# Two graph layers on one core: fp8 copies on GpSimd, layer 1's sums re-dealt over the steps, weights in one transfer, split gathers and filler matmuls

## The chip, the core and the metric

The kernel runs on one core of one Trainium2 chip. Its engines are named as the profile names them: PE is TensorE (matmuls; PEld its weight loads), DVE is VectorE, ACT is ScalarE, POOL is GpSimd, SP is SyncE. Every load of this kernel is issued by POOL, except the weights, which SP issues as it does the stores. The metric is the device time of one execution in microseconds (us). Three runs of the kernel before took 259.87, 260.9 and 263.14 us; the median is 260.9.

## What is computed

Two layers over a graph of 4096 nodes with 64 features. `adj` is a 0/1 matrix of 4096 x 4096 in float32 (64 MB), in which about one entry in 256 is set.

```python
# layer 0: the last 100 neighbours of a row count, each half of the next one
support = input @ weight
mask = (adj != 0); rank = cumsum(mask, axis=1); deg = rank[:, -1:]
k = minimum(deg, 100); pos = rank - (deg - k)
w = mask * where(pos > 0, 0.5 ** (k - pos), 0)
x = layernorm(x + (w @ support + bias))
# layer 1
deg = clip(sum(adj, axis=1) + 1, 1)
h = (adj @ x + x) / deg
out = relu(concat([x, h], axis=1) @ W + b)
x = layernorm(x + out / maximum(norm(out, axis=1), 1e-12))
```

Layer 1 needs the rows of layer 0's result, so its product `adj @ x` can only be summed over nodes that layer 0 has finished.

## The kernel before, in words

**Tiles and steps.** `adj` is cut into 8 slabs g of 512 rows (the output nodes) by 8 blocks k of 512 columns (the neighbours). A tile A[g][k] is 128 partitions x 4 x 512, loaded transposed on the host and cast from float32 to bfloat16 by the DMA (512 KB in SBUF). There are 64 steps; step i works on slab g = i // 8 and block k = 7 - i % 8, as layer 0's ranks run from the last column back.

**A step.** `weigh` makes the weights of a tile: 32 small matmuls (L294 on the tile with `tri`, L303 with the number of later neighbours `near`) into PSUM, from which ACT (L310) and DVE (L311) each turn one half into `w`. `gather` (L321) multiplies `w` by x in four matmuls, one step later, into the accumulator acc0. `count` (L264) counts the neighbours of tiles ahead, DVE adds them up as `cs` (L274, L276), `spread` (L282) sums them over the later columns and ACT makes `near` (L284). Tiles are counted in chunks: of one in slab 0, of one and two in slab 1, of two in slabs 2 and 3, of four from slab 4 on; a chunk is counted during the chunk before it, so step 30 counts the tiles of steps 32 to 35.

**Loads.** `load_next` in step i loads the tile of step i + 6 (six go ahead of step 0). The pool `a16` has 23 slots, so a load waits on POOL (L111) for a slot. POOL's other work stands in the same queue: the loads of x, the split of x into two halves of float16 (L224) in steps 0 to 7, and adding layer 0's bias (L254).

**Layer 1's sums.** Once layer 0 has finished slab k, the block k of any slab can be summed: `second` (L330), four matmuls per tile. `some_sums` does at most four matmuls a step (QUOTA), from a hand-written list `jobs` of (slab, first block, one past the last); a tile may be taken at step i if i >= 8 (k + 1) + 7 and it has been weighed. All the blocks of one job are added in acc1, an accumulator with one buffer, and `evict_part` then copies or adds it into `part[g]` on DVE (L368, L365). Jobs of the old list take 27 tiles in steps 15, 23 to 27, 31 to 34, 39 to 52 and 55 to 57. The other 37 tiles are summed in the tail.

**Kept tiles.** Tiles of slabs 0 to 3 with k >= 4 are needed again only in the tail. `keep_next` copies them to fp8 (0 and 1 are exact) in halves of 128x1024 and so frees their bf16 slot: one half a step from step 9 on but for every eighth, three on ACT (L346) to one on DVE (L344), behind the step's own work.

**Epilogue of layer 0** for slab g, by hooks in the steps after i = 8 (g + 1): in i, ACT copies acc0 (`first_hT`, L426); i + 1, PE multiplies by the weights (L432); i + 2, DVE adds x and makes the statistics (L439, L419, L421); i + 3 and i + 4, the root on ACT (L390) and DVE (L396 to L400) and the normalised x1 (L459); i + 5 and i + 6, its two halves x1hl (L464, L468, L471) and the transposes (L476); i + 7, the products with layer 1's weights (`first_pu`, L487); i + 8, `first_c1` (L496, L497). The weights themselves are scaled and split in three bfloat16 parts by DVE in steps 6 to 8 (L230 to L249).

**The tail** after step 63: layer 0's epilogue for slab 7, the sums that are left (`own`), and layer 1's epilogue in units of two slabs: `last_hT` (DVE adds part[g], L612), `last_pz` (PE, L640), `last_z` (DVE, L647), squares on ACT (L654, L655), `last_ss` (DVE, L662), the root on POOL (`last_rn`, L410), `last_y` (DVE L681, then the add on POOL, L684), `last_mv` (statistics, L419 and L421), `last_r` (POOL: L408 to L702), `last_o` (eight outputs on ACT, L722) and the stores. Slab 7 comes last, in halves of 256 columns (`own_half`, `half_hT`).

**Order.** The order of each engine's instructions is the program's, written out by hand; each engine runs its own list in that order and waits by semaphores.

```python
    def evict_part(g):
        acc = acc1.pop(g)
        if g in part:
            nc.vector.tensor_tensor(part[g], acc, part[g], ALU.add)
        else:
            part[g] = const.tile([P, R], F32, name=f"part_{g}")
            nc.vector.tensor_copy(part[g], acc)
...
    jobs = [(0, 0, 2), (1, 0, 2), (2, 0, 2), (3, 0, 3), (2, 2, 4), (0, 2, 4), (1, 2, 4)]
    jobs += [(4, 0, 4), (5, 0, 5), (6, 0, 3)]
```

Of the kernel before, what the change touches and what calls it, by code (L numbers as in the profile page):

```python
# [9 lines left out]
F32 = mybir.dt.float32  # L10
# [30 lines left out]
def adj_resnorm_kernel(  # L41
# [5 lines left out]
    w0: bass.AP,  # L47
    b0: bass.AP,
    w1: bass.AP,
    b1: bass.AP,  # L50
# [18 lines left out]
    D = w0.shape[0]  # L69
# [32 lines left out]
    def load_next(n=1, pieces=1):  # L102
        for _ in range(n):
            s = next(loads, None)
            if s is None:
                return
            g, k = s
            a = a16p.tile([P, KB, R], BF16, tag="a16", name=f"a16_{g}_{k}")
            for h in range(pieces):
                qs = slice(h * KB // pieces, (h + 1) * KB // pieces)  # L110
                nc.gpsimd.dma_start(out=a[:, qs, :], in_=adjT[g, k][:, qs, :])  # L111
            A[g][k] = a
# [14 lines left out]
    load_next(1, pieces=2)  # L127
# [58 lines left out]

    w0_sb = const.tile([P, D], F32, name="w0_sb")
    wn_sb = const.tile([P, D], F32, name="wn_sb")

    w1_sb = const.tile([P, 2 * D], F32, name="w1_sb")  # L190
    w1_parts = const.tile([P, 3, 2 * D], BF16, name="w1_parts")
# [3 lines left out]
    b0_sb = const.tile([P, D], F32, name="b0_sb")  # L195
    b1_sb = epi.tile([P, D], F32, tag="y", name="b1_sb")
# [9 lines left out]
    def load_weights():  # L206
        nc.sync.dma_start(out=w0_sb[0:D, :], in_=w0)
        nc.sync.dma_start(out=w0_sb[D:P, :], in_=w0)
        nc.sync.dma_start(out=b0_sb, in_=b0.partition_broadcast(P))
        for h in range(2):  # L210
            for c in range(2):
                nc.sync.dma_start(out=w1_sb[h * D : (h + 1) * D, c * D : (c + 1) * D], in_=w1[c * D : (c + 1) * D, :])
        nc.sync.dma_start(out=b1_sb, in_=b1.partition_broadcast(P))
        nc.sync.dma_start(out=wn_sb[0:D, :], in_=w1[D : 2 * D, :])
        nc.sync.dma_start(out=wn_sb[D:P, :], in_=w1[D : 2 * D, :])
# [13 lines left out]
    def prepare():  # L229
        nc.vector.tensor_scalar(w0_sb[0:D, :], w0_sb[0:D, :], 2.0**W_EXP, None, ALU.mult)  # L230
        nc.vector.tensor_scalar(w0_sb[D:P, :], w0_sb[D:P, :], 2.0**W_EXP / LO, None, ALU.mult)

    def prepare_last():
        nc.vector.tensor_scalar(wn_sb[D:P, :], wn_sb[D:P, :], 1.0 / LO, None, ALU.mult)
        nc.vector.tensor_scalar(w1_sb[D:P, :], w1_sb[D:P, :], 1.0 / LO, None, ALU.mult)
        for j in range(3):
            nc.vector.tensor_copy(w1_parts[:, j, :], w1_sb)
            if j < 2:
                nc.vector.tensor_tensor(w1_sb, w1_sb, w1_parts[:, j, :], ALU.subtract)

    def prepare_b1():
        for j in range(3):
            nc.vector.tensor_copy(
                b1_parts[j * 32 : j * 32 + 1], b1_sb[j * 32 : j * 32 + 1].unsqueeze(1).to_broadcast([1, TB, D])
            )
            if j < 2:
                high = epi.tile([P, D], BF16, tag="sq", name=f"b1_high_{j}")
                nc.vector.tensor_copy(high, b1_sb)
                nc.vector.tensor_tensor(b1_sb, b1_sb, high, ALU.subtract)  # L249
# [66 lines left out]
    def gather(g, k, w):  # L316
        if k == NK - 1:
            acc0[g] = ps_a.tile([P, R], F32, tag="acc0", name=f"acc0_{g}")
        for q in range(KB):
# [16 lines left out]
    def keep_next(i):  # L336
        if not to_keep:
            return
# [4 lines left out]
        if i % 4 == 3:  # L343
            nc.vector.tensor_copy(kept[g, k][:, qs, :], A[g][k][:, qs, :], saturate=False)  # L344
        else:
            nc.scalar.copy(kept[g, k][:, qs, :], A[g][k][:, qs, :], saturate=False)  # L346
# [4 lines left out]
    jobs = [(0, 0, 2), (1, 0, 2), (2, 0, 2), (3, 0, 3), (2, 2, 4), (0, 2, 4), (1, 2, 4)]  # L351
    jobs += [(4, 0, 4), (5, 0, 5), (6, 0, 3)]
    have = {g: 0 for g in range(NG)}
    acc1 = {}

    todo = [(g, b, b == k0 * KB, b == k1 * KB - 1) for g, k0, k1 in jobs for b in range(k0 * KB, k1 * KB)]
# [5 lines left out]
    def evict_part(g):  # L362
# [3 lines left out]
        else:  # L366
            part[g] = const.tile([P, R], F32, name=f"part_{g}")
            nc.vector.tensor_copy(part[g], acc)  # L368

    def some_sums(i, n):  # L370

        done = None
        while n and todo and done is None and ready(i, todo[0][0], todo[0][1]):
# [4 lines left out]
            have[g] = b // KB + 1  # L378
# [102 lines left out]
    def first_pu(g):  # L481
# [3 lines left out]
        for t in range(TB):  # L485
            for j in range(3):
                nc.tensor.matmul(  # L487
                    pu[:, t, :], lhsT=x1T[:, ts(t, P)], rhs=w1_parts[:, j, :], start=(t, j) == (0, 0), stop=False
                )
# [22 lines left out]
    at(NK - 2, DVE, prepare)  # L512
    at(NK - 1, DVE, prepare_last)
    at(NK, DVE, prepare_b1)
# [23 lines left out]
    pi = ps_m.tile([P, R], F32, tag="m", name="pi")  # L538
    for i in range(12):
        nc.tensor.matmul(pi, lhsT=idle[:, 0:P], rhs=idle, start=True, stop=True)  # L540
    pf = ps_m.tile([P, P], F32, tag="m", name="pf")
# [4 lines left out]

    nc.vector.memset(w0_sb, 0.0)
    load_weights()
    spread(0, NK - 1)
    held = None  # L550
    for c, chunk in enumerate(chunks):
# [7 lines left out]
        for (g, k), share in zip(chunk, shares):  # L559
            i = when[g, k]  # L560
            run(i, ACT)
            run(i, POOL)
            load_next()
# [7 lines left out]
            run(i, "ACT, late")  # L571
            done = some_sums(i, QUOTA)
            if share and share[-1] == ahead[-1]:
                spread(*ahead[-1])

            if i > NK and i % NK:
                keep_next(i)
            if held is not None:
                gather(*held)
# [14 lines left out]
    def own(g, b0, b1):  # L594

        for b in range(b0, b1):
            second(acc[g], g, b, b == have[g] * KB, b == NB - 1)
# [144 lines left out]
    def acc_of(g, tag, rows=R, name=None):  # L742
        return ps_a.tile([P, rows], F32, tag=tag, name=f"acc_right_{name or g}")

    acc.update({5: va[:, 0, :], 2: vb[:, 0, :], 1: va[:, 1, :], 4: vb[:, 1, :]})
    acc[0] = acc_of(0, "acc1")
    last = L * KB
    own(5, 20, 24)
# [10 lines left out]
    own(5, 24, last)  # L759
    own(2, 16, last)  # L760
    own(0, 16, 20)
    first_px(L)
    first_x1T(L)
    own(0, 20, 24)
    own(5, last, NB)
    last_hT(5)
    own(2, last, NB)
    last_hT(2)
    first_pu(L)
    first_c1(L)  # L770
# [3 lines left out]
    own(0, 24, NB)  # L774
    last_z(u)
    last_sq(u, True)
    last_hT(0)
    last_ss(u)
    last_rn(u, True)
    own(1, 16, NB)  # L780
    last_hT(1)
    last_y(u, True)
    own(4, 16, 24)
# [3 lines left out]
    own(4, 24, NB)  # L787
# [3 lines left out]
    last_sq(v, True)  # L791
    last_hT(4)
    last_ss(v)
    last_rn(v, True)
    last_o(u, 0, 8)
    store(u)
    acc[3] = acc_of(3, "acc0")
    own(3, 12, NB)
    last_y(v, True)
    last_hT(3)  # L800
    acc[6] = acc_of(6, "acc1")
    own(6, 12, 20)

    u = unit(4, 3)
    last_pz(u)
    last_mv(v)
    last_r(v, True)
    last_z(u)
    last_sq(u, True)
    last_o(v, 0, 8)  # L810
    store(v)
    own(6, 20, NB)
    last_ss(u)
    last_rn(u, True)
    last_hT(6)
    acc[L, 0] = acc_of(L, "acc0", R // 2, "7a")
    own_half(a_half, 0, NB // 4)

    v = unit(6)
    last_pz(v)  # L820
    own_half(a_half, NB // 4, NB)
    last_y(u, True)
    last_z(v)
    last_sq(v, False)
# [77 lines left out]
```

## Time and profile before

| | us |
|---|---|
| runs: median (lowest to highest) | 260.9 (259.87 to 263.14) |
| profiled execution: its time | 260.26 |
| its span, first to last instruction | 258.4 |
| busy: PE / DVE / ACT / POOL | 215.9 / 179.9 / 147.7 / 77.6 |
| ACT fp8 copies L346: 23 of 1038 ns | 23.9 |
| DVE fp8 copies L344: 9 of 693 ns | 6.2 |
| POOL load issues L111: 65 of 574 ns | 37.2 |
| POOL waiting ahead of L111 | 111.7 |
| last gather (step 63) starts | 203.58 |
| the last slab's last product (L640) starts | 247.12 |
| last output instruction ends | 255.4 |

The profile is of one execution, and its rows carry line numbers of the kernel before. Busy time of PE counts pipelined matmuls whose ends are modelled: a matmul of 512 columns is listed with 0.38 us but the next one starts 0.216 us later. The granted clock was 0.67 of full speed from 10 to 20 us and full from there to the end of the matmuls. In a timeline row the columns are start, duration, engine, line, operation, output <- input, shape and, in brackets, the idle time ahead of it and what ended it.

### The profile page before, as it was taken

What the parts mean: (1) busy time and instruction counts of PE and PEld (TensorE: products, weight loads), DVE (VectorE), ACT (ScalarE), POOL (GpSimd) and SP (SyncE); (2) the same over time, 40 slices, a digit from 0 to 9 for tenths busy, and PEclk for the clock granted to TensorE, in tenths of its full rate; (3) what the DMA queues carried; (4) which work ended last, traced back from release to release, by engine and by line L of the source; (5) the groups of instructions that cost most, each with busy time, mean ns of one, the idle gap of its engine ahead of it and who ended that gap; (6) DMA issues with size and microseconds to landing.
All of it is one profiled execution on the core that took longest, in us unless ns stands there. A gap on an engine that the chain in (4) does not pass through costs nothing.

```text
span 258.4 us, 7468 instructions
## 1 busy us (share of the span) xinstructions
PE 215.9 (84%) x3187; PEld 99.5 (39%) x3187; DVE 179.9 (70%) x471; ACT 147.7 (57%) x210; POOL 77.6 (30%) x129
## 2 busy tenths in 40 slices
PE   8496767679979996998889899998996989999920
PEld 2122224224424432442344234433442636646920
DVE  5666697796797696667957694668577555556773
ACT  5366666687878668656866575447444421064271
POOL 8655471051013240232122422130200000475640
PEclk9779999999999999999999999999999999999995
DMA  5999999999999999599899999996500000000111
GB/s 90 179 238 233 240 214 214 221 219 214 215 221 205 202 188 211 107 212 191 169 148 188 205 215 213 223 212 118 104 0 3 3 0 0 3 22 20 43 41 41
DMA packets 12241, 37.37 MB, mean 145 GB/s; under 512 B 2353, under 2 KB 3377, under 8 KB 12209
## 3 DMA queue, kind: packets, MB, share of 16 engines
q0 software_dynamic: 10128, 35.66, 69.8%
q1 hardware_dynamic: 2080, 1.25, 1.7%
q8 instruction: 25, 0.41, 0.6%
q14 instruction: 8, 0.06, 0.1%
HBM read 69.40 MB, written 1.05 MB: 273 GB/s over the span
## 4 chain that ended last, share of the span: by engine, by line
PE 37%; DMA 23%; DVE 17%; issue 9%; POOL 6%; ACT 6%; POOLq 0%; ACTq 0%; DVEq 0%
DMA a<-in_adjT_dram 23%; PE acc L321 7%; PE acc_part L330 6%; DVE w L311 4%; PE v L294 4%; ACT w L310 4%; PE acc_right L330 3%; PE cnt L264 3%; PE v L303 2%; DVE x L459 2%; POOL a L111 2%; PE pz L640 2%; PE va L330 2%; PE pu L487 2%; PE vb L330 2%
## 5 line engine op out<-in xcount | busy, mean ns | idle before, releaser
L310 ACT ACTIVATE w<-v,less 128x1024 int16<-128x1024 f32 x64 | 71.3, 1114 | 48.3 <-PE v L303 30.1
L311 DVE TENSOR_SCALAR w<-v 128x1024 int16<-128x1024 f32 x64 | 78.2, 1222 | 29.3 <-PE v L303 27.5
L111 POOL DMA_DIRECT2D a<-in_adjT_dram x65 | 37.2, 574 | 111.7 <-PE acc_part L330 36.5
L321 PE MATMUL acc<-w,xhl 128*128 128x512 bf16 x256 | 66.3, 381 | 0.2 <-ACT hT L426 0.2
L321 PEld LDWEIGHTS <-xhl 128*128 128x128 f16 x256 | 24.0, 98 | 36.6 <-issue 12.8
L294 PE MATMUL v<-a,tri 32*32 32x512 bf16 x1024 | 29.7, 390 | 6.3 <-ACT w L310 5.9
L264 PE MATMUL cnt<-a,pick 128*32 128x512 bf16 x256 | 22.9, 393 | 12.6 <-DMA a<-in_adjT_dram 12.2
L330 PEld LDWEIGHTS <-x1hl 128*128 128x128 f16 x224 | 19.6, 98 | 29.3 <-issue 10.4
L303 PE MATMUL v<-near,mine 32*32 32x512 bf16 x1024 | 29.0, 382 | 0.2 <-ACT near L284 0.2
L274 DVE TENSOR_TENSOR cs<-cnt,cs 128x512 bf16<-128x512 f32 x22 | 15.1, 688 | 18.5 <-PE cnt L264 18.5
L330 PE MATMUL acc_part<-a,x1hl 128*128 128x512 bf16 x108 | 28.0, 382 | 0.0
L284 ACT ACTIVATE near<-rep,most 128x512 bf16<-128x512 f32 x30 | 20.5, 683 | 6.6 <-PE rep L282 6.6
L346 ACT CAST a<-a 128x1024 fp8e4<-128x1024 bf16 x23 | 23.9, 1038 | 0.0
L294 PEld LDWEIGHTS <-tri 32*32 32x32 bf16 x1024 | 10.8, 88 | 28.9 <-issue 27.5
L282 PE MATMUL rep<-cs,further 128*128 128x512 bf16 x30 | 11.8, 392 | 9.8 <-DVE cs L274 7.4
L410 POOL TENSOR_TENSOR rn<-ss,power 128x8 f32<-128x8 f32 (+1 forms) x4 | 6.0, 1506 | 34.8 <-DVE ss L664 34.7
L264 PEld LDWEIGHTS <-pick 128*32 128x32 bf16 x256 | 5.3, 94 | 28.6 <-issue 19.4
L330 PE MATMUL acc_right<-a,x1hl 128*128 128x512 fp8e4 (+1 forms) x56 | 12.9, 379 | 0.0
L654 ACT ACTIVATE sq<-z 128x512 f32<-128x512 f32 x3 | 1.9, 630 | 17.2 <-DVE z L647 17.2
L419 DVE BATCH_NORM_STATS2 st_l<-y 128x6 f32<-128x64 f32 x60 | 9.0, 214 | 1.0 <-POOL y L684 0.8
L303 PEld LDWEIGHTS <-mine 32*32 32x32 bf16 x1024 | 9.3, 88 | 0.8 <-issue 0.7
L464 ACT CAST x1hl<-x 128x256 f16<-128x256 f32 x8 | 3.2, 405 | 10.6 <-DVE x L459 10.6
(135 smaller groups left out, 255.8 us busy)
## 6 DMA issues: line engine op xcount, KB each, us to landing
a<-in_adjT_dram POOLq DMA_DIRECT2D x63, 512.0 KB, 9.3
c<-in_x_quads_dram POOLq DMA_DIRECT2D x8, 128.0 KB, 11.8
x<-in_x_dram POOLq DMA_DIRECT2D x8, 128.0 KB, 9.3
out_dram<-o SPq DMA_DIRECT2D x8, 128.0 KB, 1.7
a<-in_adjT_dram POOLq DMA_DIRECT2D x2, 256.0 KB, 4.9
w_sb<-in_L_gnn_W_dram SPq DMA_DIRECT2D x4, 16.0 KB, 10.8
w_sb<-in_L_gnn_weight_dram SPq DMA_DIRECT2D x2, 16.0 KB, 6.2
b_sb<-in_L_gnn_bias_dram SPq DMA_DIRECT2D x1, 32.0 KB, 8.2
```

Source lines behind the costliest of these rows:

```text
L111: nc.gpsimd.dma_start(out=a[:, qs, :], in_=adjT[g, k][:, qs, :])
L264: nc.tensor.matmul(cnt[g][quarters[q], :], lhsT=pick[:, PW - 4 * k : PW - 4 * k + Q], rhs=A[g][k][:, q, :], start=first, stop=last,)
L274: nc.vector.tensor_tensor(new, cnt[g], cs[g], ALU.add)
L282: nc.tensor.matmul(pr, lhsT=further, rhs=cs[g], start=True, stop=True)
L284: nc.scalar.activation(near[g], pr, AF.Relu, bias=most, scale=-1.0)
L294: nc.tensor.matmul(v[e // 2][quarters[q], e % 2, :], lhsT=tri[quarters[e], :], rhs=A[g][k][quarters[e], q, :], start=True, stop=False,)
L303: nc.tensor.matmul(v[e // 2][quarters[q], e % 2, :], lhsT=mine[quarters[e], 4 * k + q, :], rhs=nr[quarters[e], :], start=False, stop=True,)
L310: nc.scalar.activation(w[:, 0:2, :], v[0], AF.Relu, bias=less)
L311: nc.vector.tensor_scalar(w[:, 2:4, :], v[1], -STEP * MAX_NEIGH, 0.0, ALU.add, ALU.max)
L321: nc.tensor.matmul(acc0[g], lhsT=xhl[:, b, :], rhs=w[:, q, :].bitcast(BF16), start=(k, q) == (NK - 1, 0), stop=(k, q) == (0, KB - 1),)
L330: nc.tensor.matmul(acc, lhsT=x1hl[:, b, :], rhs=A[g][b // KB][:, b % KB, :], start=first, stop=last)
L346: nc.scalar.copy(kept[g, k][:, qs, :], A[g][k][:, qs, :], saturate=False)
```

## The change

It has seven parts:

- `keep_next` runs on POOL alone, ahead of the step's load, from step 3 on and only for tiles already weighed: one half a step, steps 3 to 34.
- `jobs` lists single blocks in any order; 20 jobs take 39 tiles in steps 15, 16, 23 to 26, 30 to 35 and 37 to 63. A slab's first eviction is an ACT copy, the later ones are DVE adds.
- The tail sums what is left (`left`, 25 tiles) in a new order, with other accumulators; the last unit of layer 0 (`first_pu`, `first_c1` of slab 7) comes later in it.
- The four weight arrays become one array of 128x384, put together on the host and loaded by one SP transfer in step 1; POOL scales and splits it in steps 6 and 9 to 12.
- The first tile is loaded in one transfer, not two halves.
- In a step that ends a chunk and has no sums, half of the gather goes ahead of `spread`.
- Filler matmuls: 14 instead of 12 ahead of the start, and 4, 2, 4 and 3 more around the first counts and step 0.

```diff
-    load_next(1, pieces=2)
+    load_next()
...
     def load_weights():
-        nc.sync.dma_start(out=w0_sb[0:D, :], in_=w0)
...
-        nc.sync.dma_start(out=wn_sb[D:P, :], in_=w1[D : 2 * D, :])
+        nc.vector.memset(wts[:, 0:1], 0.0)
+        nc.sync.dma_start(out=wts, in_=weights)
...
-    def prepare_last():
-        nc.vector.tensor_scalar(wn_sb[D:P, :], wn_sb[D:P, :], 1.0 / LO, None, ALU.mult)
...
+    def prepare_w1(j):
+        if j == 0:
+            low = wts[D:P, D : 4 * D]
+            nc.gpsimd.tensor_scalar(low, low, 1.0 / LO, None, ALU.mult)
+        nc.gpsimd.tensor_copy(w1_parts[:, j, :], w1_b1)
+        if j < 2:
+            nc.gpsimd.tensor_tensor(w1_b1, w1_b1, w1_parts[:, j, :], ALU.subtract)
...
-    def gather(g, k, w):
+    def gather(g, k, w, q0=0, q1=KB):
...
     def keep_next(i):
-        if not to_keep:
+        if i < 3 or not to_keep or when[to_keep[0][0:2]] >= i:
             return
...
-        if i % 4 == 3:
-            nc.vector.tensor_copy(kept[g, k][:, qs, :], A[g][k][:, qs, :], saturate=False)
-        else:
-            nc.scalar.copy(kept[g, k][:, qs, :], A[g][k][:, qs, :], saturate=False)
+        nc.gpsimd.tensor_copy(kept[g, k][:, qs, :], A[g][k][:, qs, :], saturate=False)
...
-    jobs = [(0, 0, 2), (1, 0, 2), (2, 0, 2), (3, 0, 3), (2, 2, 4), (0, 2, 4), (1, 2, 4)]
-    jobs += [(4, 0, 4), (5, 0, 5), (6, 0, 3)]
+    jobs = [(0, [0]), (1, [0])]
+    jobs += [(2, [0, 1]), (0, [1]), (1, [1])]
+    jobs += [(3, [1, 0, 2]), (0, [2]), (1, [2]), (2, [2]), (4, [2, 1, 0, 3])]
+    jobs += [(0, [3]), (1, [3]), (2, [3]), (5, [3, 2, 1, 0, 4]), (3, [3, 4])]
+    jobs += [(6, [4, 3, 2, 1, 0, 5]), (4, [4, 5]), (0, [4, 5]), (1, [4, 5]), (2, [4])]
...
             part[g] = const.tile([P, R], F32, name=f"part_{g}")
-            nc.vector.tensor_copy(part[g], acc)
+            nc.scalar.copy(part[g], acc)
...
+    at(1, DVE, load_weights)
-    at(NK - 2, DVE, prepare)
-    at(NK - 1, DVE, prepare_last)
-    at(NK, DVE, prepare_b1)
+    at(NK - 2, POOL, prepare)
+    for j in range(3):
+        at(NK + 1 + j, POOL, prepare_w1, j)
+    at(NK + 4, POOL, prepare_b1)
...
+    def warm(n):
+        a = A[0][NK - 1][:, 0, :]
+        for i in range(n):
+            nc.tensor.matmul(pi, lhsT=a[:, 0:P], rhs=a, start=True, stop=True)
...
             run(i, POOL)
+            keep_next(i)
             load_next()
...
+            n_todo = len(todo)
             done = some_sums(i, QUOTA)
+            half = 0
             if share and share[-1] == ahead[-1]:
+                if held is not None and len(todo) == n_todo:
+                    half = KB // 2
+                    gather(*held, 0, half)
                 spread(*ahead[-1])
-            if i > NK and i % NK:
-                keep_next(i)
+            if i == 0:
+                warm(3)
             if held is not None:
-                gather(*held)
+                gather(*held, half)
```

The new tail from the last sums of slab 5 on, in program order:

```python
    last_hT(5); own(2, 7); last_hT(2); own(0, 7)
    u = unit(5, 2)
    last_pz(u); last_hT(0); last_z(u); last_sq(u, True)
    own(1, 7); last_hT(1); last_ss(u); last_rn(u, True); own(4, 7)
    v = unit(0, 1)
    last_pz(v); last_hT(4); last_z(v); last_sq(v, True)
    own(3, 7); last_hT(3); last_y(u, True); last_ss(v); last_rn(v, True)
    own(6, 6, 7)
    w = unit(4, 3)
    last_pz(w); last_mv(u); last_r(u, True); last_z(w); last_sq(w, True)
    last_o(u, 0, 8); store(u); last_y(v, True); last_ss(w); last_rn(w, True); last_hT(6)
    own_half(a_half, 0, NB // 4)
    u, v, y = v, unit(6), w
    last_pz(v); first_pu(L); first_c1(L); own_half(a_half, NB // 4, NB)
    last_mv(u); last_r(u, True); last_z(v); last_sq(v, False); last_o(u, 0, 8); store(u)
    last_y(y, True); last_ss(v); last_rn(v, True)
    half_hT(a_half); own_half(b_half, 0, NB // 2)
```

## The prediction

> **What bounds the kernel now.** I read four views in this order: the page's busy slices, the waits, the timelines of PE, ACT, DVE and POOL, and the groups by shape. The slices first.
>
> ```profile
> PE   8496767679979996998889899998996989999920
> DMA  5999999999999999599899999996500000000111
> POOL 8655471051013240232122422130200000475640
> ```
>
> The load queue is full (9) for the first 16 slices (0 to 103 us), dips, and is empty from 190 us. PE has gaps until 60 us, few later, and is full in the tail (204 to 247 us) until the last slab's epilogue. So: a stage paced by loads, a stage paced by PE, a tail paced by PE. POOL is nearly idle in the middle. The waits and PE's timeline show where PE's own time goes.
>
> ```profile
> POOL a L111 <- PE acc_part L330: 36.5, 17, 7.4
> POOL a L111 <- ACT a L346: 30.2, 9, 6.9
> PE cnt L264 <- DMA a<-in_adjT_dram: 12.2, 15, 2.0
> ...
> 103.15 0.40 PE L264 MATMUL cnt<-a,pick 128*32 128x512 bf16 x4 [2.04 <-DMA a<-in_adjT_dram]
> 104.56 1.02 PE L321 MATMUL acc<-w,xhl 128*128 128x512 bf16 x4
> ...
> 148.75 1.03 PE L321 MATMUL acc<-w,xhl 128*128 128x512 bf16 x4
> ...
> 172.90 1.03 PE L321 MATMUL acc<-w,xhl 128*128 128x512 bf16 x4
> ```
>
> A load (L111) waits for a slot that a sum or an fp8 copy must free; PE then waits for the load. Between 148.75 and 172.90 us PE waits for almost nothing: eight steps, each with a sum, take 24.15 us, 3.02 a step. The last six steps, without sums, take (203.58 - 190.50)/6 = 2.18 (gathers of steps 57 and 63). A sum inside the stage thus costs 0.84 us, about its four matmuls (4 x 216 ns = 0.86). It is not free there.
>
> **The change, part by part**, against the profiled execution: span 258.4 us, time 260.26, so 1.9 outside the span; the median of the runs, 260.9, is 0.6 above it.
>
> *Slots.* The load at step i brings tile i+6, so the n-th load is in step n-7 and needs n-23 slots freed. Step 30 counts tile 35 (the 36th load), which needs 13 freed. Before, slots come free in steps 10, 12, 14, 15, 17, 19, 21, 23, 23, 24, 25, 26, 26: the 13th in step 26. After, in 4, 6, 8, 10, 12, 14, 15, 16, 16, 18, 20, 22, 23: step 23. Three steps of some 2.8 us are 8 us, against a median of 9.3 from issue to landing. The wait at 103.15 and the 0.40 ahead of it go: -2.4. Before that, up to 55 us, the queue is full whatever PE does, so the 4 us of small weight work that leaves DVE (L230 to L249, 178 to 390 ns each) buys nothing: PE would wait for DMA instead (1.10 at 50.16). The first tile as one transfer saves one issue (0.55) ahead of everything: -0.5. The weights' nine issues on SP had no other work behind them; their one transfer is used from step 6 on. Filler matmuls and gather halves lie in waits for DVE (1.54 at 9.27, 0.2 in later steps) under the load pace: 0, and 13 x 0.216 = 2.8 if they did not. Sum up to step 29: -2.9.
>
> *Copies on POOL.* 32 half tiles (128x1024) leave ACT (23 x 1038 ns) and DVE (9 x 693 ns), which were not the bound. POOL has no such row. The lower end is DVE's own cast of that shape, 0.7 us. The upper is L224 (two inputs, 128x256 in 678 ns) as a pure rate, 2.7. Between them stands POOL's iota, 128x128 in 259 ns, about 100 of it fixed (a 128x1 memset): 1.24 ns an element, 1.4 us for 1024. A copy has one input more than that and one fewer than L224; I take 1.4, by the row that streams without a second operand. Per step POOL then spends 1.4 + 0.55 (load) + 0.16 (L125 and L254 over eight steps) = 2.1, below the 2.42 at which 0.524 MB tiles arrive (217 GB/s over 60 to 80 us). The weights' split adds 11 small operations in steps 6 and 9 to 12, some 4 us by DVE's rows above, which POOL's idle half of 40 to 60 us (5 of 20 us busy) covers. A copy stays hidden up to 1.7; behind it in POOL's queue stand the loads, the split L224 that feeds the gather, and L254. The Trainium skill ("GPSIMD Engine Reference", 4.1 Engine selection) says that one-input work is roughly at line rate on GpSimd; at its 1.03 cycles an element and 1.2 GHz my estimate from that page is 0.9 us. No row here shows it.
>
> A rule against the copies has a row:
>
> ```profile
> 53.01 0.72 POOL L254 TENSOR_TENSOR x<-x,b_sb 128x256 f32<-128x256 f32 x1 [7.00 <-DMA x<-in_x_dram]
> 53.15 0.60 DVE L400 SCALAR_TENSOR_TENSOR r_l<-s_l,q_l 128x4 f32<-128x4 f32 x1
> 149.96 0.16 DVE L400 SCALAR_TENSOR_TENSOR r_l<-s_l,q_l 128x4 f32<-128x4 f32 x1
> ```
>
> The same tiny DVE operation takes 0.16 us alone and 0.60 beside POOL: it ends when POOL ends. The skill's "SBUF — State Buffer", Who interferes with whom, states it: a DVE instruction with two SBUF inputs is locked out by a GpSimd instruction that reads SBUF. Steps 3 to 34 hold the epilogues of slabs 0 to 2 with some five such operations each; each can lose up to a copy. Much of it lies in DVE's slack (7 to 9 of 10 us busy): I take +0.5, with ends 0 and 15 x 1.4 = +21.
>
> *Sums re-dealt.* 39 tiles instead of 27 are summed before the tail. Up to step 29 both have six. From step 30 to 63 the old kernel has 21 in 34 steps and took 203.58 - 104.56 = 99.0 us, loads included. The new one has 33, plus one step without: 33 x 3.02 + 2.2 = 101.9. So +2.9, loads no longer in the way (28 tiles after the 36th at 2.42 land by 170 us).
>
> *Evictions.* The accumulator acc1 has one buffer. There are now 20 jobs instead of 10, so the first matmul of the next one waits for evict_part. Before, jobs ended in steps with little else on DVE (i mod 8 = 7, 1, 3). Now they also end in steps 32, 40, 48, 56, where ACT does hT first, and 34, 42, 50, 58, 60, where DVE does an epilogue first.
>
> ```profile
> 136.50 0.59 ACT L426 COPY hT<-acc 128x512 f32<-128x512 f32 x1 [0.61 <-PE acc L321]
> 136.98 1.04 PE L330 MATMUL acc_part<-a,x1hl 128*128 128x512 bf16 x4
> 143.24 0.36 DVE L421 BATCH_NORM_AGGREGATE mv_l<-st_l 128x2 f32<-128x6 f32 x4
> 143.48 1.04 PE L330 MATMUL acc_part<-a,x1hl 128*128 128x512 bf16 x4
> ```
>
> Step 40: hT ends at 137.09, an ACT copy of some 0.6 more (128x512 took 586 ns in L426) ends at 137.7, the sum stood ready at 136.98: 0.8 lost, four times. Step 42: statistics end at 143.60, the add (L365, 683 ns) at 144.3, the sum was ready at 143.48: 0.9, four times. Step 60: behind it stand L396 to L459 (1.8 instead of 1.3) and no rep: 1.5. Sum 8.3; behind each waiting sum are the gather and the next step's matmuls, so it all counts, less some 0.2 a step of waits for w (0.24 at 152.97) that it covers: I take +7. Ends 0 and +9.
>
> *Tail.* 12 tiles fewer x 0.864 = -10.4 of PE. I laid the new order out by the rows, in us from the last gather (203.58). PE now arrives early and waits twice. First, slab 6's hT stands on DVE behind unit 5_2: pz ends 14.3, z 15.3, squares on ACT (2 x 630 ns) 16.6, hT4 and the next z between, y 20.4, POOL's add 21.2, statistics 23.2, z, y, ss 26.3, hT 26.9. PE was there at 23.1: 3.8 lost. Second, the last slab's first half_hT stands on ACT behind the eight outputs of unit 0_1: pu 28.8, c1 29.8, statistics 31.6, POOL's root and offset (L408 to L702, 2.6) 34.3, outputs (2.76) 37.2, hT 37.6. PE was there at 33.5: 4.1 lost. Then pz, 16 matmuls and hT: the last product starts at 40.6, against 43.54 in the trace (247.12) and 44.4 for the old order laid out likewise. So -2.9 to -3.8: I take -3.4, with ends -10.4 and 0.
>
> Sum: -2.9 + 0.5 + 2.9 + 7 - 3.4 = +4.1; span 262.5, time 264.4, 1.3% above the median.
>
> **The rivals.** *The sums move for free.* The evictions fall into waits and the tail keeps its full cut: 4.1 - 7 - 7 = -9.9, time 250. For it: the freed slots, and ACT and DVE lose 30 us of copies. Against it: 3.02 a step is PE's own work, and the two rows on each eviction. *POOL becomes the bound.* A copy of 2.2 us makes its step 2.9, 0.5 above the load pace, 32 times: +16, less the 8 us by which loads are now early: +8, time 272; at 2.5, 282. It decides from about 1.95, where 32 x (1.95 + 0.71 - 2.42) eats the 8. For it: L224's rate. Against it: a second input is gone. *DVE locked out.* Copies in front of x1 (L459) delay x1hl and w in steps 12, 20 and 28: about 2 us each, +6, time 270. For it: the row at 53.15; against it: DVE's slack. *The change does not do what it says:* slots free no earlier because a copy waits on POOL behind L254 (7 us at 53.01); then -2.4 is lost, time 267.
>
> **How the numbers follow.** The forecast has 0.48, free sums 0.17, POOL bound 0.16, lock-out 0.12, late slots 0.07. About 2% tells this kernel from no change: 255.7 to 266.1. Of the forecast's own spread (evictions 0 to 9, tail -10.4 to 0) 0.05 lies above that and 0.02 below. Faster 0.19, same 0.41, slower 0.40. The range leaves a tenth at each end: 252 (half of free sums) to 275 (half of POOL bound); the forecast's own is 257.5 to 267.
>
> **What would show it.** Right: no DMA wait at the counts near 100 us; POOL copies of 0.9 to 1.7 us with loads still back to back; eight steps with sums at 3.0 plus 1.7 of waits of acc_part for ACT and DVE at the named steps; PE idle twice for about 4 us in the tail, before slab 6's pz and before the last slab's first pz. Wrong: copies above 1.9 with DMA dips before 100 us; x1 rows that stretch beside copies; sums that start on time after an eviction.

## The result: 5.7% slower

The changed kernel takes 275.98 us (median of 4 runs, 275.31 to 277.06), the kernel before 261.18 on the same chip (4 runs): ratio 1.057, 95% interval 1.052 to 1.063. The prediction was 264.4, its range 252 to 275. The profiled execution took 275.57, its span is 273.8. Two views of it first: busy slices, then waits (us in total, times, longest).

```profile
PE   7776886808996999998999899989987999939360
...
PEclk9999999786998999999999999999999999977775
DMA  6999999999999999999999999810000000001101
```

The load queue stays full to 170 us, so the late loads near 100 us are gone, as forecast. But PE has a hole in the 9th slice (55 to 62 us) and others in the tail, and behind each the granted clock is down. (It is down in the 8th slice too, ahead of the hole: see the tail's part of "Why the prediction was wrong".)

```profile
ACT x1hl L447 <- DVE x L442: 22.5, 8, 8.1
...
PE v L277 <- ACT w L293: 11.6, 5, 7.7
...
PE cnt L247 <- DMA a<-in_adjT_dram: 8.1, 11, 1.6
...
PE vc L602 <- DVE hT L613: 4.6, 1, 4.6
...
PE acc_part L313 <- DVE part L349: 4.2, 5, 1.4
...
PE pz_7a L641 <- ACT hT L620: 4.1, 1, 4.1
...
PE acc_part L313 <- ACT part L352: 2.9, 5, 0.6
```

PE's waits for loads (`cnt`) all lie before 60 us. Those for `vc` and `pz_7a` are the forecast waits of the tail (3.8 and 4.1 us), and PE's waits for evictions (`acc_part`) come to 7.1, where 8.3 of waits, and 7 of time, were forecast. The first two lines are not forecast at this size: PE waits 11.6 us for ACT's half of `w`, and ACT stood in front of it waiting for DVE's `x1`. POOL's copies themselves are short:

```profile
L327 POOL CAST a<-a 128x1024 fp8e4<-128x1024 bf16 x32 | 33.4, 1045 | 0.1
L442 DVE TENSOR_SCALAR x<-y,mv_l,r_l 128x64 f32<-128x64 f32 x32 | 12.6, 458 | 0.3
```

```profile
L459 DVE TENSOR_SCALAR x<-y,mv_l,r_l 128x64 f32<-128x64 f32 x32 | 7.9, 312 | 0.3
```

A copy takes 1.045 us (forecast 1.4; the estimate of 0.9 from the Trainium skill, "GPSIMD Engine Reference", 4.1 Engine selection, was nearer). Its victim is the second row: in the kernel before, the same 32 operations of DVE took 7.9 us (third row). Here is the place, in the timeline of DVE, POOL, ACT and PE:

```profile
54.09 1.89 DVE L383 SCALAR_TENSOR_TENSOR r_l<-s_l,q_l 128x4 f32<-128x4 f32 x1
...
55.84 1.05 POOL L327 CAST a<-a 128x1024 fp8e4<-128x1024 bf16 x1
56.01 5.05 DVE L442 TENSOR_SCALAR x<-y,mv_l,r_l 128x64 f32<-128x64 f32 x4
...
57.35 1.05 POOL L327 CAST a<-a 128x1024 fp8e4<-128x1024 bf16 x1
...
61.15 0.41 ACT L447 CAST x1hl<-x 128x256 f16<-128x256 f32 x1 [8.07 <-DVE x L442]
61.46 1.11 ACT L293 ACTIVATE w<-v,less 128x1024 int16<-128x1024 f32 x1
...
62.62 0.66 PE L277 MATMUL v<-a,tri 32*32 32x512 bf16 x16 [7.67 <-ACT w L293]
```

Four operations of 128x64 take 5.05 us, beside copies that come every 1.5 us here, not one in a step; the tiny two-input operation just ahead of them takes 1.89 us, where the prediction's row of it alone shows 0.16. Behind them stand ACT's high half of `x1`, then `w`, then PE. The same chain follows from step 20 to 21, with a shorter wait:

```profile
87.19 0.66 PE L277 MATMUL v<-a,tri 32*32 32x512 bf16 x16 [2.66 <-ACT w L293]
```

Where the two kernels part is seen best at the end of ACT's `w`, once in each step (us; the last two columns are the time from step 63's `w` to the end of the span, and the span; the later rows are the experiments below):

| | step 9 | 13 | 20 | 30 | 63 | tail | span |
|---|---|---|---|---|---|---|---|
| before | 41.01 | 56.31 | 74.19 | 105.40 | 203.24 | 55.2 | 258.4 |
| after | 39.89 | 62.57 | 82.15 | 113.74 | 217.74 | 56.1 | 273.8 |
| e1 after, copies on ACT and DVE | 39.94 | 55.67 | 74.56 | 105.27 | 209.19 | 56.6 | 265.8 |
| e2 before, copies on POOL | 48.78 | 67.62 | 87.53 | 116.20 | 209.87 | 55.1 | 265.0 |
| e3 after, x loaded early | 40.37 | 59.10 | 78.63 | 112.89 | 216.87 | 56.6 | 273.5 |
| e9 after, x1 on ACT | 39.82 | 56.76 | 74.77 | 110.78 | 216.51 | 55.1 | 271.6 |
| e5 e1, evictions first | 39.90 | 55.59 | 74.98 | 104.87 | 203.58 | 56.6 | 260.2 |
| e7 e1, tail's order | 40.14 | 55.83 | 74.73 | 105.44 | 209.35 | 53.0 | 262.3 |
| e8 e1, old jobs and tail | 39.93 | 55.65 | 74.47 | 104.71 | 198.01 | 55.2 | 253.2 |
| e10 e7, more of the tail's order | | | | 105.89 | 209.81 | 50.2 | 260.0 |
| e11 e10, evictions first | | | | 104.97 | 203.68 | 50.2 | 253.9 |
| e12 before, copies early | | | | 105.01 | 198.59 | 55.1 | 253.7 |

### The profile page after: what moved, and what is told of

It is laid out like the page before. It is cut to its first block, busy times and chain, and to the rows that moved or that the text cites. A ratio compares the mean times of both kernels' runs of the same rounds, so it can differ in the third digit from the quotient of the medians.

```text
span 273.8 us, 7491 instructions
## 1 busy us (share of the span) xinstructions
PE 223.5 (82%) x3202; PEld 102.6 (37%) x3202; DVE 185.8 (68%) x449; ACT 131.9 (48%) x194; POOL 111.5 (41%) x171
## 3 DMA queue, kind: packets, MB, share of 16 engines
HBM read 69.40 MB, written 1.05 MB: 257 GB/s over the span
## 4 chain that ended last, share of the span: by engine, by line
PE 52%; DVE 20%; DMA 11%; POOL 7%; ACT 6%; issue 4%; ACTq 0%; DVEq 0%; POOLq 0%
PE acc L304 13%; PE acc_part L313 12%; DMA a<-in_adjT_dram 11%; PE v L277 6%; DVE w L294 4%; PE cnt L247 4%; DVE x L442 4%; PE v L286 4%; PE pu L470 2%; POOL a L327 2%; ACT w L293 2%; PE pz L415 2%; PE va L313 2%; DVE st_l L402 2%; POOL a L106 1%
## 5 line engine op out<-in xcount | busy, mean ns | idle before, releaser
L304 PE MATMUL acc<-w,xhl 128*128 128x512 bf16 x256 | 70.9, 389 | 1.4 <-DVE xhl L213 1.2
L106 POOL DMA_DIRECT2D a<-in_adjT_dram x64 | 35.1, 549 | 58.3 <-PE acc_part L313 36.5
L313 PE MATMUL acc_part<-a,x1hl 128*128 128x512 bf16 (+1 forms) x156 | 40.3, 381 | 7.1 <-DVE part L349 4.2
L277 PE MATMUL v<-a,tri 32*32 32x512 bf16 x1024 | 29.8, 394 | 11.9 <-ACT w L293 11.6
L327 POOL CAST a<-a 128x1024 fp8e4<-128x1024 bf16 x32 | 33.4, 1045 | 0.1
L247 PE MATMUL cnt<-a,pick 128*32 128x512 bf16 x256 | 21.2, 389 | 8.8 <-DMA a<-in_adjT_dram 8.1
L277 PEld LDWEIGHTS <-tri 32*32 32x32 bf16 x1024 | 10.1, 88 | 35.4 <-issue 34.0
L237 POOL TENSOR_TENSOR x<-x,wts 128x256 f32<-128x256 f32 x8 | 5.8, 725 | 27.3 <-DMA x<-in_x_dram 27.2
L442 DVE TENSOR_SCALAR x<-y,mv_l,r_l 128x64 f32<-128x64 f32 x32 | 12.6, 458 | 0.3
L723 ACT ACTIVATE o<-y,off,r 128x64 f32<-128x64 f32 x20 | 6.9, 427 | 9.2 <-POOL off L703 9.2
```

The costliest lines, as they stand in the source:

```text
L106: nc.gpsimd.dma_start(out=a, in_=adjT[g, k])
L247: nc.tensor.matmul(cnt[g][quarters[q], :], lhsT=pick[:, PW - 4 * k : PW - 4 * k + Q], rhs=A[g][k][:, q, :], start=first, stop=last,)
L277: nc.tensor.matmul(v[e // 2][quarters[q], e % 2, :], lhsT=tri[quarters[e], :], rhs=A[g][k][quarters[e], q, :], start=True, stop=False,)
L304: nc.tensor.matmul(acc0[g], lhsT=xhl[:, b, :], rhs=w[:, q, :].bitcast(BF16), start=(k, q) == (NK - 1, 0), stop=(k, q) == (0, KB - 1),)
L313: nc.tensor.matmul(acc, lhsT=x1hl[:, b, :], rhs=A[g][b // KB][:, b % KB, :], start=first, stop=last)
L327: nc.gpsimd.tensor_copy(kept[g, k][:, qs, :], A[g][k][:, qs, :], saturate=False)
```

## The experiments

Line numbers of a variant can differ by some from those of its parent. The ratios are to the kernel before on the same chip; the kernel before itself had medians of 260.9 to 262.8 us on them, so half a per cent between variants on different chips says little, and the profiles decide.

### Who holds x1: e1, e2 and a measurement by itself (e4)

e1 gives the copies, and nothing else, back to ACT and DVE:

```diff
             run(i, POOL)
-            keep_next(i)
             load_next()
...
+            keep_next(i)
             if i == 0:
                 warm(3)
...
-        nc.gpsimd.tensor_copy(kept[g, k][:, qs, :], A[g][k][:, qs, :], saturate=False)
+        if i % 4 == 3:
+            nc.vector.tensor_copy(kept[g, k][:, qs, :], A[g][k][:, qs, :], saturate=False)
+        else:
+            nc.scalar.copy(kept[g, k][:, qs, :], A[g][k][:, qs, :], saturate=False)
```

> The changed kernel with the fp8 copies alone given back to ACT (three of four) and DVE, at the end of the same steps 3 to 34. Lock-out theory (the 7.7 us and the 2.7 us that PE waits for ACT's w in steps 13 and 21 come from DVE's x1 group held by POOL's copies): the x1 group of slab 0 goes from 5.05 us back to about 1, both waits go, and the time falls by 9 to 11.5, to 264.5 to 267. Rival (loads pace this part anyway, and the loss sits in the sums and the tail): PE waits for the loads instead, the time falls by less than 4, to 272 or more.

267.95 us, ratio 1.021 (1.015 to 1.027), against 1.057. The x1 group of slab 0 in the timeline of DVE, and PE's waits for `w`:

```profile
53.14 1.02 DVE L445 TENSOR_SCALAR x<-y,mv_l,r_l 128x64 f32<-128x64 f32 x4
```

```profile
PE v L277 <- ACT w L293: 3.3, 8, 1.1
```

1.02 us and not 5.05; PE's waits for ACT's `w` fall by 8.3 us (11.6 to 3.3), and step 63 comes 8.55 us earlier, somewhat less than expected. So the copies on POOL cost 8.5 us more than the same copies on ACT and DVE, through those waits. Loads did not take their place: PE waits 9.1 us for them, 8.1 in the changed kernel.

e2 is the kernel before with `keep_next` as in the change (on POOL, ahead of the load, from step 3), its other parts left out.

> The kernel before with one part of the change alone: the copies on POOL ahead of the load, steps 3 to 34. Lock-out theory: the waits for x1 in steps 12 and 20 appear here too; +8 to +11 for them and -2.4 for the load wait at step 30 that the earlier slots remove, so 267 to 270. Rival (the loss sits in the sums and the tail): 258 to 262.

266.80 us, ratio 1.017 (1.011 to 1.022): the time is near the theory's, but not by its path. Of the 13.3 us lost by step 20, 7.8 are there at step 9 already. In the kernel before, DVE splits the weights in steps 7 and 8, and these operations are held too; the timelines of DVE, before and e2:

```profile
35.16 0.35 DVE L235 TENSOR_SCALAR w_sb<-w_sb 64x128 f32<-64x128 f32 x1
35.55 0.23 DVE L237 CAST w_parts<-w_sb 128x128 bf16<-128x128 f32 x1
```

```profile
37.79 1.19 DVE L235 TENSOR_SCALAR w_sb<-w_sb 64x128 f32<-64x128 f32 x1
39.01 1.36 DVE L237 CAST w_parts<-w_sb 128x128 bf16<-128x128 f32 x1
```

The stall in e2 is in PE's timeline:

```profile
43.67 0.59 PE L282 MATMUL rep<-cs,further 128*128 128x512 bf16 x1 [7.27 <-DVE cs L274]
```

So with the copies on POOL the weights' move from DVE to POOL avoids a stall of 7 to 8 us in step 9. Less is left of that at the end. e12 below makes the same copies in the same steps on ACT and DVE, and at step 63 e2 is 11.3 us behind it (209.87 against 198.59), where the changed kernel is 8.5 behind e1. So the copies on POOL cost 11.3 us with the weights on DVE and 8.5 with them on POOL, and the move is worth some 2.7 us (an estimate: the two pairs differ in other parts too). Without copies on POOL it is worth about nothing (e8 and e12 below). The prediction priced it by itself.

e4 measures the disputed cost without the kernel, in one execution. Each kind of DVE operation runs alone, then from the moment POOL starts eight copies back to back:

```python
    for fn, n in kinds:
        nc.vector.memset(back, 0.0)
        nc.gpsimd.tensor_tensor(gate, back, less, ALU.add)
        for i in range(8):
            h = slice(2 * (i % 2), 2 * (i % 2) + 2)
            nc.gpsimd.tensor_copy(a8[:, h, :], a[:, h, :], saturate=False)
        nc.vector.tensor_copy(less, gate)
        fn(n)
```

> No part of the reference is computed: six kinds of DVE operation run first alone and then beside a train of eight fp8 copies on POOL, and one kind on ACT beside the train. Lock-out theory: the form of x1 (128x64 f32, two scalars from SBUF) goes from about 0.25 us to 0.8 to 1.1 each, as one fits between two copies; the small operation with two SBUF inputs (0.16) and the f32 tensor_tensor (0.41) go to about 1 too; statistics and the read from PSUM stay, ACT stays. If only memory bandwidth is shared, each is stretched by the same small factor, under 1.5.

The timeline, first alone, then each beside its train (x12 is the number of operations, so the second column is their sum):

```profile
3.18 2.76 DVE L64 TENSOR_SCALAR x<-y,mv,r 128x64 f32<-128x64 f32 x12 [0.93 <-DMA y<-in_x_dram]
...
11.64 1.61 DVE L76 BATCH_NORM_STATS2 st<-y 128x6 f32<-128x64 f32 x12
...
20.59 3.65 DVE L84 COPY b<-a 128x1024 bf16<-128x1024 bf16 x8
...
24.45 7.93 POOL L101 CAST a<-a 128x1024 fp8e4<-128x1024 bf16 x8
24.62 8.69 DVE L64 TENSOR_SCALAR x<-y,mv,r 128x64 f32<-128x64 f32 x12
...
54.97 1.61 DVE L76 BATCH_NORM_STATS2 st<-y 128x6 f32<-128x64 f32 x12
...
72.07 9.26 POOL L101 CAST a<-a 128x1024 fp8e4<-128x1024 bf16 x8
...
72.24 9.38 DVE L84 COPY b<-a 128x1024 bf16<-128x1024 bf16 x8
...
82.89 4.08 ACT L89 ACTIVATE xa<-y,less,r 128x64 f32<-128x64 f32 x12
```

x1's form goes from 2.76 to 8.69: eight operations at one for each copy (7.93), four at 0.23. The small two-input operations go from 2.31 to 8.56 for twelve. It is not bandwidth: statistics stay as they are, six reads from PSUM take 7.50 and 7.51, ACT 0.34 each (eight outputs in the tail take 2.76, the same). The f32 `tensor_tensor` goes from 0.45 to 1.17 each, and so, which was not foreseen, does the bf16 copy with a single input (0.46 to 1.17); both stretch the train from 7.93 to 9.26, as if the two engines took turns.

The prediction used one sentence of the Trainium skill ("SBUF — State Buffer", Who interferes with whom), that a DVE instruction with two SBUF inputs is locked out. The same list says that copies, casts and `tensor_scalar` in a two-port mode contend too, and x1, the weights' split and the bf16 copy are of these forms: e4 and e2 agree with it, though no view shows the mode itself.

### Spacing the copies, or moving the victim: e3 and e9

e3 asks whether the copies hurt because POOL, after waiting 7 us for x, catches up:

```diff
-        at(NK * g + 3, POOL, load_x, g)
+        at(NK * g if g else 3, POOL, load_x, g)
```

> The changed kernel with the loads of x for slabs 1 to 7 issued three steps earlier, so that POOL does not wait 7 us for them. Theory 'burst' (copies hold DVE only because they come back to back, 1.05 of every 1.55 us, after that wait): POOL is paced by the loads, one copy in some 2.4 us, the x1 group of slab 0 takes 1.5 to 2.5 us, and the time falls by 6 to 10, to 266 to 270. Note that the x of slab 0 is loaded as before, so one wait of POOL is left. Rival (any copy holds DVE for its own length, however it is spaced): x1 still takes 4 us or more, the time stays above 273.

273.72 us, ratio 1.042 (1.035 to 1.050): neither, as the time is the rival's and the length of x1 the theory's. The profile is of its slowest run (275.26). POOL no longer waits for x from slab 1 on, and around x1 of slab 0 the copies still come every 1.5 us (timeline of POOL):

```profile
57.79 1.05 POOL L327 CAST a<-a 128x1024 fp8e4<-128x1024 bf16 x1
58.77 0.53 POOL L106 DMA_DIRECT2D a<-in_adjT_dram  x1
59.29 1.05 POOL L327 CAST a<-a 128x1024 fp8e4<-128x1024 bf16 x1
```

Nothing paces POOL while slots are free: it runs ahead of the steps at its own 1.05 + 0.53 us, denser than the 2.4 of the loads that the prediction reckoned with. Only from 66.5 to 78.9 us, when it waits ahead of most loads, do the copies come every 2.1 to 2.9 us, and no x1 falls there: what the pace alone costs is not shown. The x1 group took 1.72 us here and 1.70 in e2, with one of its four operations held (1.05 us), where in the changed kernel all four were (1.08, 1.45, 1.06 and 1.70) at the same pace of copies. How they fall among the copies may decide it; no run shows that. At step 13 it stands 2.8 us behind the kernel before and not 6.3, but from step 20 to 24 it loses 4.3 more, the changed kernel 2.3.

e9 leaves the copies on POOL and makes x1 on ACT:

```diff
-        at(i + 4, DVE, first_x1, g)
+        at(i + 4, DVE, first_x1_act, g)
...
+        nc.vector.scalar_tensor_tensor(off, mv[:, :, 0], -1.0, r, ALU.mult, ALU.mult)
+        for t in range(TB):
+            nc.scalar.activation(
+                x1[:, g * TB + t, :], y[:, t, :], AF.Identity, bias=off[:, t : t + 1], scale=r[:, t : t + 1]
+            )
```

> The changed kernel with its copies on POOL, but x1 of slabs 0 to 6 is made on ACT (four operations with bias and scale) and not by the four two-scalar operations on DVE; DVE makes the bias, one small operation of two SBUF inputs. Lock-out theory by the reader's side: the 5.05 us of x1 in step 12 are gone, four small operations of DVE that POOL still holds stay (some 1 us each), so the wait of 7.7 us falls to 3 to 4.5 and the time by 3 to 6 against the changed kernel (ratio to the kernel before 1.0574): 1.035 to 1.046. Rival (the wait in step 13 is set by POOL or the loads and x1 only shows it): ratio 1.052 or more.

273.98 us, ratio 1.049 (1.042 to 1.055), between the two. In slab 0 it does what the theory says: step 20 ends at 74.77, 7.4 us ahead of the changed kernel. From the end of step 20 to that of 24 it loses 6.2 us of that against the kernel before. There four small two-input operations stand in a row on DVE beside copies and take 1.17, 1.04, 1.13 and 0.95 us; DVE's half of `w` stands behind them, and PE waits for it (timelines of DVE and PE):

```profile
76.06 1.04 DVE L380 SCALAR_TENSOR_TENSOR q_l<-q_l,eps_ln,mv_l 128x4 f32<-128x4 f32 x1
...
80.64 0.39 PE L277 MATMUL v<-a,tri 32*32 32x512 bf16 x2 [3.50 <-DVE w L294]
```

One of the four, the bias, and the 1.43 us of x1 on ACT are this variant's own, so not all of the 6.2 us is due to the operations that stayed. Taking one victim away is not enough where a chain has several.

### Evictions: e5

```diff
             held = (g, k, w)
+            if done is not None:
+                evict_part(done)
             if g > 0 and k == NK - 1:
                 first_hT(g - 1)
             run(i, PE)
             run(i, DVE)
-            if done is not None:
-                evict_part(done)
```

> Like e1_copies_back, and the eviction of acc1 stands ahead of first_hT on ACT and of the epilogue on DVE (before the step's hooks, not after them). In e1_copies_back PE waits 8.0 us for evictions in ten places. Theory (those waits are on the path, as the prediction's eviction term has it): most of them go, -5 to -7 against e1_copies_back, ratio to the kernel before 0.995 to 1.002. Rival (the waits hide waits for w that would be there anyway): -2 or less, ratio 1.013 or more.

262.02 us, ratio 1.003 (1.000 to 1.006), 1.8% below e1. Step 63 comes 5.6 us earlier than in e1 with the tail unchanged. The eviction waits of e1 (8.0 us, first two lines) are nearly gone in e5 (third line):

```profile
PE acc_part L313 <- DVE part L352: 4.2, 5, 1.4
PE acc_part L313 <- ACT part L355: 3.8, 5, 1.2
```

```profile
PE acc_part L313 <- ACT part L355: 1.1, 2, 0.8
```

They were on the path: 6.9 us less waiting, 5.6 us of time, inside the 5 to 7 expected (the ratio lies just above its band).

### The tail: e6, e7, e10, e11

The timeline of PE in the changed kernel's tail:

```profile
245.75 1.87 PE L602 MATMUL vc<-a,x1hl 128*128 128x256 bf16 x8 [4.61 <-DVE hT L613]
...
253.08 1.91 PE L602 MATMUL vd<-a,x1hl 128*128 128x256 bf16 x16
259.11 1.11 PE L641 MATMUL pz_7a<-wts,hT 128*128 128x64 f32 x4 [4.11 <-ACT hT L620]
260.01 3.62 PE L602 MATMUL vd<-a,x1hl 128*128 128x256 bf16 x16
264.09 0.66 PE L641 MATMUL pz_7b<-wts,hT 128*128 128x64 f32 x4 [0.46 <-ACT hT L620]
```

Both waits are the forecast ones in place and nearly in length (hT of slab 6 ends at 26.8 us after the last gather; forecast 26.9). But slab 7's eight matmuls (L602) stand behind the first wait, because their accumulator is the other half of slab 6's tile `vc`, and the matmuls after each wait are slow: the granted clock is 0.50 from 245 to 250 us and from 259 to 264. Sixteen matmuls take 3.62 us there (line of 260.01) and 1.91 at full clock (line of 253.08). e6 gives slab 7 banks of its own:

```diff
-    acc[L, 0] = vc[:, 1, a_half]
-    acc[L, R // 2] = vd[:, 0, a_half]
+    acc[L, 0] = ps_a.tile([P, R // 2], F32, tag="acc1", name="acc_right_7a")
+    acc[L, R // 2] = ps_a.tile([P, R // 2], F32, tag="acc0", name="acc_right_7b")
```

> Like e1_copies_back, and slab 7's first half is summed in a PSUM tile of its own, not in the second half of the tile vc that slab 6 uses. Theory (the wait of 4.6 us stands ahead of slab 7's eight matmuls only because they share a tile with slab 6, whose hT is read late): the eight matmuls go into that wait, the wait moves to slab 6's product and is 3.5, -1 to -2 in all, ratio 1.013 to 1.017. Rival (nothing changes, because the wait is for hT of slab 6 in any case and DVE sets the end): -0.5 or less, 1.019 or more.

266.16 us, ratio 1.021 (1.018 to 1.025). The wait is 3.83 us and the tail of the profiled execution 2.6 us shorter than e1's, but the ratio is e1's: inconclusive. e7 adds the order:

```diff
     own(6, 6, 7)
+    last_hT(6)
...
-    last_hT(6)
...
     first_pu(L)
-    first_c1(L)
     own_half(a_half, NB // 4, NB)
-    last_mv(u)
-    last_r(u, True)
     last_z(v)
     last_sq(v, False)
+    last_ss(v)
+    last_rn(v, True)
+    first_c1(L)
+    last_mv(u)
+    last_r(u, True)
+    half_hT(a_half)
     last_o(u, 0, 8)
```

> Like e6_own_bank, and in the tail DVE takes hT of slab 6 as soon as its sums are there, the first unit's statistics after it, c1 of slab 7 behind z, squares and sums of unit 6, and ACT takes slab 7's first hT ahead of the eight outputs. Theory (the two waits of some 4 us are an order of DVE and ACT, and the clock falls behind them): both go, the last product starts some 41 us after the last gather and not 45, -6 to -9 against e1_copies_back, ratio 0.987 to 0.998. Rival (DVE's own work from 230 us on sets the end, and the waits only show it): -3 or less, ratio 1.010 or more.

264.34 us, ratio 1.014 (1.011 to 1.017): 0.7% below e1, less than half of what was expected, and in the rival's band. But the two waits are gone and came back as one (timeline of PE):

```profile
240.67 1.91 PE L605 MATMUL acc_right_7b<-a,x1hl 128*128 128x256 bf16 x16
250.67 1.11 PE L644 MATMUL pz_7b<-wts,hT 128*128 128x64 f32 x4 [8.08 <-ACT hT L623]
```

ACT's hT of the second half now stands behind outputs of unit 4_3, which wait for POOL. e10 reorders the rest, of which the main lines are shown: both hT ahead of the outputs, unit 4_3's add on POOL ahead of unit 0_1's root, unit 6's y in a buffer of its own, its outputs on DVE.

```diff
+    last_y(y, True)
     last_rn(v, True)
     first_c1(L)
...
+    half_hT(b_half)
...
     last_o(u, 0, 8)
...
-    last_y(v, True)
+    last_y(v, True, epi.tile([P, TB, D], F32, tag="near", name="y1_6"))
...
-    last_o(v, 0, 4)
+    last_o(v, 0, 4, on_act=False)
```

> Like e7_tail_order, in which the two waits came back as one of 8.1 us ahead of the last product, with both hT of slab 7 on ACT ahead of the outputs, POOL's add of unit 4_3 ahead of the root of unit 0_1, unit 6's y in a buffer of its own, and its outputs on DVE. Theory (after the last sums the tail is the chain of the units' epilogues through DVE, POOL and ACT in their written order, and not PE's matmuls): -5 to -8 against e7_tail_order, ratio 0.984 to 0.995. Rival (DVE's work is the bound whatever the order): -2 or less, ratio 1.006 or more.

261.37 us, ratio 1.000 (0.997 to 1.003), again 1.4% less and again short of the expectation, but beyond the rival's band: the order does count. The last product now starts at 243.51, but the span ends at 260.0: 16.5 us later, against 11.3 in the kernel before. e11 is e10 with e5's evictions.

> e10_tail_chain with the evictions first, as in e5_evict_first, which was worth 1.8% by itself. If the two add, ratio 0.967 to 0.978, which would make the re-dealt sums worth having: e8_old_deal, with the old jobs and tail, is at 0.9785. If the tail then waits for something that the evictions had covered, 0.985 or more.

255.93 us, ratio 0.979 (0.974 to 0.984): the gains of e5 and e10 add, just short of the expected band. Busy time in its tail, by stretches (PE, PEld, DVE, ACT, POOL, each with its number of instructions; then the granted clock):

```profile
226.90:238.00 11.10, 10.05 (x95) 8.76 (x94) 9.22 (x48) 4.65 (x12) 9.44 (x12) 1.00 0.08 26
238.00:253.90 15.90, 0.04 (x1) 0.00 (x0) 9.71 (x59) 6.76 (x20) 6.77 (x12) 0.62 0.15 50
```

PE is done at 238; what is left is the epilogue on DVE, POOL and ACT. So with twelve tiles less in the tail its end is no longer set by PE but by the epilogue, where no engine is busy for more than 9.7 of the 15.9 us, and 10.4 us of PE bring 5.0 in the best order tried (55.2 to 50.2).

### What the rest of the change is worth: e8 and e12

e8 is e1 with `jobs`, `evict_part` and the tail of the kernel before.

> Like e1_copies_back, with the jobs, the evictions and the tail of the kernel before: what is left of the change are earlier slots, weights in one transfer split on POOL, split gathers and filler matmuls. Theory (the re-dealt sums with their evictions and the tail cost e1_copies_back its 5 us): 258 to 261 where the kernel before is at 261 to 262.8, ratio 0.985 to 0.998. Rival (the weights on POOL or the fillers cost something): ratio 1.005 or more.

255.04 us, ratio 0.979 (0.976 to 0.982): faster than expected. e12 changes one thing in the kernel before, the steps in which the copies are made:

```diff
-        if not to_keep:
+        if i < 3 or not to_keep or when[to_keep[0][0:2]] >= i:
...
-            if i > NK and i % NK:
-                keep_next(i)
+            keep_next(i)
```

> The kernel before with one thing changed: its fp8 copies, still on ACT and DVE, are made in steps 3 to 34, one half a step, and not in steps 9 to 42. e8_old_deal, which has this and the weights in one transfer, the split gathers and the filler matmuls, is 5.2 us ahead of the kernel before at step 63, most of it won in steps 30 to 47. Theory (earlier slots alone: the loads of steps 30 to 47 are no longer late, and ACT and DVE are free of copies from step 35 on): -4 to -5.5, ratio 0.979 to 0.985. Rival (weights, gather halves or fillers won it): ratio 0.992 or more.

255.83 us, ratio 0.980 (0.975 to 0.986), inside the theory's band. Between 95 and 165 us PE waits 6.2 us for loads in six places in the kernel before and nowhere in e12. So earlier copies alone win 2%, and weights, split gathers and fillers together about nothing (step 63 at 198.59 here, 198.01 in e8).

## Why the prediction was wrong, step by step

From the table, the 15.4 us of the two spans split, with the prediction's terms beside them:

| | predicted | measured | from |
|---|---|---|---|
| slots, first tile, sums re-dealt | 0.0 (-2.9 + 2.9) | +0.4 (-5.2 + 5.6) | e8 - before; e5 - e8, at step 63 |
| evictions | +7 | +5.6 | e1 - e5, at step 63 |
| POOL's copies hold DVE | +0.5 | +8.5 | after - e1, at step 63 |
| tail | -3.4 | +0.9 | last two columns |
| sum | +4.1 | +15.4 | |

- *Failed: "Much of it lies in DVE's slack: I take +0.5".* The mechanism was named, with its row and as a rival of 270 us with 0.12, and its place was right (steps 12 and 20; step 28 has no copy left beside it). The price was 8.5 us and not 0.5. The runs show three things that it had wrong. The slack is not where the operations are: x1 stands in a chain x1, high half, `w`, PE (timeline above; e1 takes the waits away). More forms are held than those with two SBUF inputs (e4). And the copies are not one in a step but one in 1.5 us in many places; how much of the price is due to that pace no run tells. The measured 8.5 lie within the ends 0 and 21 that the prediction had; the value between was chosen on the slack, with no row that showed the slack at that place.
- *Failed: the tail* (-3.4 forecast, +0.9 measured). Both waits were foreseen to within 0.8 us, but the last product starts 45.2 us after the last gather and not 40.6. Of these 4.6 us, 2.5 are there when ACT's hT of slab 7's first half ends (40.1 against 37.6), the others come behind it. Two things fit this. The clock behind the waits was left out: sixteen matmuls took 1.7 us longer than at full clock. And eight matmuls that share a tile with slab 6 came behind the first wait. The Trainium skill ("TensorE: Matmul & The Clock Gate", HAM oscillation — how this bites in real kernels) has the rule that gaps over some 3.4 us throttle TensorE; behind the gaps here of 7.7, 4.6 and 4.1 us the clock was 0.50. But these traces do not keep to that figure: the clock was 0.50 too behind the wait of 2.66 us (87 to 90 us), and from 49 to 52 us behind two load waits of 0.78 and 1.60 us with four matmuls between them, while no eviction wait by itself (up to 1.4 us) lowered it. Of the 10.4 us at the forecast's lower end the best order tried won 5.0; e11's span ends with 15.9 us in which PE has nothing to do.
- *Right in the sum by luck, not in its parts: slots and sums.* e5 has both with the copies on ACT and DVE and most eviction waits gone. At step 30 it is 0.5 us ahead of the kernel before, where -2.9 was forecast: the load wait at 103.15 is gone, but at step 24 the variants with early copies (e1, e5, e8, e12) are 0.7 to 1.4 us behind the kernel before. From step 30 to 63 it takes 98.7 us against 97.8: +0.9, where +2.9 was forecast. The two errors cancel. Split by parts of the change instead, earlier slots are worth 5.2 (e8), 4.3 of them in steps 31 to 47, where the loads were late too; and re-dealt sums cost 5.6 (e5 - e8), about half of the 10.4 us of matmuls that 12 tiles take. Which of PE's waits took in the other half is not shown.
- *Right: evictions* (8.3 of waits and 7 of time forecast, 7.1 and 5.6 measured), *copies hidden in POOL's own time*, *no DMA wait near 100 us*. The rival "POOL becomes the bound" falls with 1.045 us a copy. The 1.4 forecast for a copy had some luck: the iota row of 259 ns that it rests on is the shortest of three of that shape (511 and 518 ns are the others), and by the longer ones the same sum gives over 3 us.
- *Incomplete: "buys nothing" for the weights.* True alone; with the copies on POOL it avoids a stall of 7 to 8 us in step 9 (e2), of which some 2.7 are left at step 63.

## What to carry to other kernels

Before work moves to GpSimd, list the vector engine's operations of the same stretch by form: in these runs every copy, cast, `tensor_scalar` or two-input form with SBUF operands that was tried beside GpSimd copies was held for about a whole GpSimd instruction, and statistics, reads from PSUM and ScalarE were not; price it where a chain hangs on them, not by mean slack. Ask what paces the queue that the work moves to: it ran ahead while it had slots and put many copies only 1.5 us apart. And shifting work out of a stage pays only to the next bound: test the change's parts one by one, here the earlier steps of the copies alone (e12) won 2%, and the whole change is 8% slower than that.

## What was not expected of the hardware

- A DVE copy of bf16 with a single input, 0.46 us alone, takes 1.17 beside POOL's copies and slows them in turn by 17% (7.93 to 9.26 us).
- One thing stays open: the third x1 operation of slab 0 took 1.06 us (from 58.38) while POOL only issued two loads, and L383 (1.89 us) and the fourth (1.70) ended only after the load issue that followed a copy; in the kernel before, four such operations took 1.02 beside load issues. So what holds an operation longer than one copy is not known.
